# A bidirectional minGRU with a ternary feed-forward: order of the first loads, the place of one scale, the engine of small statistics, and the last steps

## The chip, the cores and the metric

The kernel runs on one core of one Trainium2 chip. The metric is the device time of one execution in microseconds (us); the figure shown is the median of several runs. Profiles come from one further, profiled execution.

## What is computed

The input x has shape (8, 512, 512): eight sequences b of 512 tokens with 512 features. The reference, cut to what matters:

```python
# _layernorm(v) has neither scale nor shift; all weights of the recurrence are ctx_1024[i], all biases cond_1024[i]
def mingru(x, W, b):                     # W, b serve for z and for h_tilde, in both directions
    z = sigmoid(x @ W.T + b);  h_tilde = tanh(x @ W.T + b)
    a = clip(1 - z, 1e-8, 1 - 1e-8)
    return linear_scan(a, z * h_tilde)   # h[s] = a[s] * h[s-1] + (z * h_tilde)[s]

def stack(x):                            # 4 layers
    h = x
    for i in range(4):
        h_new = mingru(h, ctx_1024[i], cond_1024[i])
        if i > 0: h_new = h_new + h
        h = layernorm(h_new) * gamma + beta
    return h

xn = _layernorm(x)
h = concat(stack(xn), flip(stack(flip(xn))))          # forward and backward in time
x = x + h @ fusion_W.T + fusion_b
y = _layernorm(x)
h = gelu(y @ absmean(W_fc).T)                         # 512 -> 2048, exact gelu
h = layernorm(h) * ln_w + ln_b                        # over the 2048
return x + h @ absmean(W_proj).T                      # 2048 -> 512
# absmean(W): sign(W) where |W| is over half the mean of |W|, 0 elsewhere
```

## The kernel before

**Layout.** P is 128. A sequence in the recurrence lies as features on partitions and its 512 tokens along the free dimension: four chunks of 128 features (NC_ = 4), each 128x512. Layer norms run over features, so a chunk group is turned by TensorE to four row tiles of 128 tokens (NT = 4), normalised, and turned back.

**One layer of one sequence and direction** (`layer`, L537). For each output chunk o: `gates` (L456) issues four matmuls into u (L461, 128x512, contracted over four input chunks); ScalarE makes a, t and z out of u (L478–L480); VectorE clips a (L484), multiplies z by t (L485) and scans (L489). For layers after the first the residual is added (L548 or L554). `norm` then queues two kinds of pieces: `turns`, four of them, each four transposes into a PSUM tile pt (L316, the pool of pt has two buffers), then `stats` and `normalise` (L168–L189) giving one token tile tok; and `backs`, four transposes of the four tok tiles into pf (L325), copied by ScalarE to h or x^T with gamma and beta (L331). After the last layer only the reciprocal deviation is taken (`norm_last`).

**Statistics of a row tile** (`stats`, `normalise`): bn_stats (L171) and bn_aggr (L173) on VectorE; ve = variance + eps (L177, VectorE); rs = ve to the power −0.5 (L178, GpSimd); nmu = −mean (L182, VectorE); nmr = nmu · rs (L188, ScalarE); tok = rs · src + nmr (L189, ScalarE). The same two functions serve for rows of x (rs alone), for the last layer (rs alone) and for rows of the feed-forward's input y.

**The first layer and x's own layer norm.** x is loaded twice: as rows (xn), for statistics, and transposed (x^T, `xT`), for the matmuls. The mean is taken out of the first weights instead of x: column means of the weights come from matmuls with ones into pm (L708), and four VectorE instructions subtract them from gw[0] (L711). The reciprocal deviations rx of a sequence are turned and spread by four transposes into pr (`scale_x`, L367) and copied by ScalarE to `scale` (L371). `first_layer` (L491) makes four chunks per sequence: four matmuls into u (L504); then, in a later stage, z = u · scale (L511), the factors, product, forward scan and backward scan. The statistics of a row can be made by ScalarE instead of VectorE (`second`, L375: two passes with accumulation, L380 and L382, one small operation between, and an end on VectorE and GpSimd, L385 and L386); `norm_x(b, at, scalar)` says for which rows.

**What sets the order.** The program order of each engine is written by hand (`manual_schedule`). `slot` (L439) is the unit: it issues the matmuls of one chunk, then the stages that are due ("factors", "late", "scans", "resid"), and between them shares of the queues `turns`, `backs`, `xturns` and `xbacks`; the ends of what they issued (normalise, copies to h) go last. A stage is put on the list with the slot number at which it is due (`now[0]` counts slots). [...]

**The start.** Twelve loads of 256 KB for sequence 0 go out from the queues of ScalarE and SyncE, first weights (`first_gw`), rows (`load_x`) and x^T (`first_xT`) mixed; then SyncE's queue issues the rest in turn. VectorE makes constants; two x rows' statistics are taken before the weights' fold (L711), the others after it. Chunk 0's matmuls are followed at once by pr (`with_scale`, L722).

**Feed-forward.** The weights have been made ternary during the recurrence. For each of 8 · 16 steps j, `fc(b, k)` makes 128 hidden features of one sequence (ph, gelu g, its square, high and low parts ghi and glo), sums g and its square for the layer norm, and two steps later `proj` adds them into four PSUM tiles po, one for each row tile. `token_stats(b)` turns the sums into rs and nmr per token (pow L882, nmrg L886). For the last sequence `center` (L896) adds the shift to the four rows before po is done, and `finish_last` (L915–L918) scales po, adds and stores one row tile; it is called after the last matmuls of each row tile. Near the end (L939) two steps issue `fc` twice, so that the last `proj` calls come row tile by row tile.

Of the kernel before, what the change touches and what calls it, by code (L numbers as in the profile page):

```python
# [24 lines left out]
def kernel(  # L25
# [68 lines left out]
    def load_x(use, b, t):  # L94
        xs[use, b, t] = xsp.tile([P, H], F32, tag="xs", name=f"x{use}_{b}_{t}")
        nc.sync.dma_start(out=xs[use, b, t], in_=x[b, ts(t, P), :])
# [10 lines left out]
    gb = const.tile([P, L, NC_], F32, name="gb")  # L107
    gam = const.tile([P, NC_], F32, name="gam")
    bet = const.tile([P, NC_], F32, name="bet")
    fb = const.tile([P, H], F32, name="fb")  # L110
    lnw = const.tile([P, NF], F32, name="lnw")
    lnb = const.tile([P, NF], F32, name="lnb")

# [2 lines left out]
    nc.vector.memset(warm, 0.0)  # L116
    ones = const.tile([P, P], F32, name="ones")
    nc.vector.memset(ones, 1.0)
    both = const.tile([P, NC_, 2, 64], F32, name="both")
    picks = []  # L120
    for i in range(2):
        s = const.tile([P, P], F32, name=f"fpick{i}")
        nc.vector.memset(s, 0.0)
        nc.vector.memset(s[64 * i : 64 * i + 1, :], 1.0 / H if i else 1.0)
        picks.append(s)
# [4 lines left out]
    def first_gw(q, c):  # L130
        q.dma_start(out=gw[0][:, c, :], in_=gru_wT[0][ts(c, P), :])

    def first_xT(q, c):
        q.dma_start(out=xT[0][:, c, :], in_=xt[0][ts(c, P), :])

    first_gw(nc.scalar, 0)
    load_x("n", 0, 0)
    first_gw(nc.scalar, 1)
    load_x("n", 0, 1)
    first_gw(nc.scalar, 2)  # L140
    first_gw(nc.sync, 3)
    first_xT(nc.scalar, 0)
    load_x("n", 0, 2)
    first_xT(nc.scalar, 1)
    load_x("n", 0, 3)
    for c in range(2, NC_):
        first_xT(nc.sync, c)
    nc.sync.dma_start(out=gb, in_=gru_b)
    for t in range(NT):
        load_x("n", 1, t)  # L150
# [17 lines left out]
    def stats(src, name, rs=None, shift=True):  # L168

        st = small.tile([P, 6], F32, tag="st", name=f"st_{name}")  # L170
        nc.vector.bn_stats(st, src)  # L171
        mv = small.tile([P, 2], F32, tag="mv", name=f"mv_{name}")
        nc.vector.bn_aggr(mv, st)  # L173
        if rs is None:
            rs = small.tile([P, 1], F32, tag="rs", name=f"rs_{name}")
        ve = small.tile([P, 1], F32, tag="ve", name=f"ve_{name}")
        nc.vector.tensor_scalar(ve, mv[:, 1:2], LN_EPS, None, ALU.add)  # L177
        nc.gpsimd.tensor_tensor(rs, ve, mhalf, ALU.pow)  # L178
        if not shift:
            return rs, None  # L180
        nmu = small.tile([P, 1], F32, tag="nmu", name=f"nmu_{name}")
        nc.vector.tensor_scalar(nmu, mv[:, 0:1], -1.0, None, ALU.mult)  # L182
        return rs, nmu

    def normalise(dst, src, rs_nmu, name):
        rs, nmu = rs_nmu
        nmr = small.tile([P, 1], F32, tag="nmr", name=f"nmr_{name}")
        nc.scalar.activation(nmr, nmu, AF.Copy, scale=rs)  # L188
        nc.scalar.activation(dst, src, AF.Identity, bias=nmr, scale=rs)  # L189

    def ternary(dst, w, hi_lo):
# [37 lines left out]
    with rec:  # L229
# [53 lines left out]
        def take(q):  # L283
            _, _, key, go = q.pop(0)
            left[key] -= 1
            return go()
# [104 lines left out]
        def norm_x(b, at, scalar=()):  # L391
            rx[b] = small.tile([P, NT], F32, tag="rsv", name=f"rx_{b}")
            for t in range(NT):
                queue(xturns, ("x", b), at + t, 0, second(b, t) if t in scalar else tokens(
                    lambda t=t: xs["n", b, t], None, rx[b][:, t : t + 1], f"x{b}_{t}"))
            queue(xbacks, ("x", b), at + NT + (2 if scalar else 1), 0, scale_x(b))
# [90 lines left out]
        def scan(dst, a, z, backward):  # L487
            d = slice(None, None, -1) if backward else slice(None)
            nc.vector.tensor_tensor_scan(dst[:, d], a[:, d], z[:, d], 0.0, ALU.mult, ALU.add)  # L489

        def first_layer(b, lag=0):  # L491


            zf, zb = [], []

            def chunk(o):
                def work():
                    while zlive[0] + 2 > ZT:
                        slot(None, 2)
                    zlive[0] += 2  # L500
                    name = f"{b}_0_{o}"
                    u = ps_u.tile([P, S], F32, tag="u", name=f"u_{name}")
                    for c in range(NC_):
                        nc.tensor.matmul(  # L504
                            u, lhsT=gw[0][:, c, ts(o, P)], rhs=xT[b][:, c, :],
                            start=(c == 0), stop=(c == NC_ - 1),
                        )

                    def scaled():
                        z = zp.tile([P, S], F32, tag="z", name=f"z_{name}")  # L510
                        nc.vector.tensor_tensor(z, u, scale[b], ALU.mult)  # L511
                        a, t = factors(z, z, 0, o, name)

                        def scans():
                            product(a, z, t)
                            f = zp.tile([P, S], F32, tag="z", name=f"zf_{name}")
                            scan(f, a, z, False)
                            zf.append(f)
                            if o == NC_ - 1:
                                state[b, 0] = xT.pop(b)  # L520
                                norm((b, 0), zf, f"{b}0_0", 2 if b == 1 else 1, 2 if b < 2 else 1)

                            def backward():
                                scan(z, a, z, True)
                                zb.append(z)
                                if o == NC_ - 1:
                                    norm((b, 1), zb, f"{b}1_0", 2 if b == 1 else 1, 2 if b < 2 else 1)
                            if b == 0:
                                stages.append((now[0] + 1, "resid", backward))
                            else:  # L530
                                backward()
                        stages.append((now[0] + 1, "scans", scans))
                    stages.append((now[0] + lag, "factors", scaled))
                return work
            return [chunk(o) for o in range(NC_)]

# [158 lines left out]
                load_x(use, b, t)  # L695


        norm_x(0, -2, (2,))
        norm_x(1, -2, (2, 3))
        for _ in range(2):  # L700
            take(xturns)

        idle = ps_t.tile([P, H], F32, tag="pt", name="idle")
        for _ in range(9):
# [5 lines left out]
            w = gw[0][:, c, :]  # L710
            nc.vector.scalar_tensor_tensor(w, pm0, -1.0 / H, w, ALU.mult, ALU.add)  # L711

        two = take(xturns)
        stages.clear()
        take(xturns)
        two()
        nc.vector.tensor_scalar(ngb, gb, -1.0, None, ALU.mult)
        take(xturns)
        f0, f1 = first_layer(0), first_layer(1, 2)
        first = f0[0]  # L720

        def with_scale():  # L722
            first()
            take(xbacks)()
        f0[0] = with_scale
        for i, work in enumerate(f0 + f1):
            slot(work, 4 if i == NC_ + 1 else 2, i > NC_ + 1)
        for i, v in enumerate((bet, gam)):
# [62 lines left out]


    gpool = ctx.enter_context(tc.tile_pool(name="g", bufs=3, reuse_waits="tile"))
    partp = ctx.enter_context(tc.tile_pool(name="parts", bufs=5, reuse_waits="tile"))
    accp = ctx.enter_context(tc.tile_pool(name="acc", bufs=1, reuse_waits="tile"))
    ps_x = ctx.enter_context(tc.tile_pool(name="ps_x", bufs=2, space=PSUM, reuse_waits="tile"))
    ps_o = ctx.enter_context(tc.tile_pool(name="ps_o", bufs=1, space=PSUM, reuse_waits="tile"))
# [116 lines left out]

    def finish_last(b, t):  # L915
        row = xs["y", b, t]
        nc.vector.scalar_tensor_tensor(row, po[b][t], stat[b][0][:, t : t + 1], row, ALU.mult, ALU.add)
        store(b, t)  # L918

    rests = []  # L920
    found, ytok = {}, {}
# [14 lines left out]
    for j in range(ends):  # L936
        b, k = divmod(j, NF)
        late = []
        for _ in range(2 if ends - 4 <= j < ends - 2 else 1):  # L939
            if todo:  # L940
                waiting.append((*todo[0], *fc(*todo[0])))
                todo.pop(0)
        if j == ends - 2:
            late.append(token_stats(b))
        if k == 0 and b > 0:
            late.append(token_stats(b - 1))
        if b == 0 and 5 <= k < 5 + NC_ + 3:
            row_piece(k - 5)
        if b + 1 < B and k >= NF - NC_:
            px = ps_x.tile([P, S], F32, tag="px", name=f"py_{b + 1}_{k}")  # L950
            late.append(y_chunk(b + 1, ytok[b + 1], k - (NF - NC_), px))
        if j >= LAG:
            done = waiting.pop(0)
            proj(*done)
        for f in late:
            f()
        if rests:
            rests.pop(0)()
        if j >= LAG and done[1] == NF - 1:
            finish(done[0])  # L960
        at = 12 if b == 0 else 8
        if at <= k < at + NT:
            xt = xs["y", b, k - at]
            nc.vector.tensor_tensor(xt, xt, rows[1], ALU.add)
        if b + 1 < B:
            if k == 2:
                load_y(b + 1)
            if k in (6, 7):
                y_stats(b + 1, (2 * k - 12, 2 * k - 11))
            if k in (8, 9):  # L970
                y_tokens(b + 1, (2 * k - 16, 2 * k - 15))
# [47 lines left out]
```

## Time and profile before

| what | value |
|---|---|
| median of 3 runs | 1719.33 us (1719.25 to 1719.43) |
| the profiled execution | 1719.44 us, its span 1717.4 us |
| instructions | 19766 |
| granted TensorE clock | 1.0 |
| pow of the statistics, L178 with tok following | 192 of them, median 655 ns, 548 to 1454 |
| nmr on ScalarE, L188 | 192, median 294 ns |
| tok on ScalarE, L189 | 192, median 777 ns |
| GpSimd's busy time | 214.5 us in 334 instructions |
| DMA | 91.75 MB, mean 53 GB/s |

The span is the time from the first to the last instruction that the profile shows; the time of an execution holds some 2 us more. Rows of the profile give line, engine, operation, out<-in by the program's names, shape, and how often; then busy time and the mean length of one. A timeline row gives start and length in us. A row of stretches gives the stretch, its length, and for PE, weight loads, VectorE, ScalarE and GpSimd the busy time and, in brackets, the number of instructions. A row of waits gives who waits for whom: us in total, times, longest.

### The profile page before, as it was taken

The numbers are of one execution on the slowest core, as the hardware profiler recorded it, in microseconds if no ns is written. First come the engines' busy times: TensorE is split into PE (matmuls) and PEld (weight loads), VectorE is DVE, ScalarE is ACT, GpSimd is POOL, SyncE is SP. The second block draws the span as 40 slices with busy tenths as digits, with TensorE's granted clock in tenths as the row PEclk, the third lists the DMA queues.
The fourth block names the chain that finished last, engine by engine and source line by source line (L and its number), as shares of the span: only waits on it lengthen the run. The fifth ranks groups of instructions, "written<-read, shape, count | busy, mean of one in ns | idle before, by whom it ended". The sixth has DMA issues, their size and how long they took to land.

```text
span 1717.4 us, 19766 instructions
## 1 busy us (share of the span) xinstructions
PE 1705.8 (99%) x6442; PEld 1042.8 (61%) x6442; DVE 1449.8 (84%) x2859; ACT 1072.3 (62%) x1851; POOL 214.5 (12%) x334
## 2 busy tenths in 40 slices
PE   9999999999999999999999999999999999999998
PEld 4455554555555455555545555554688888888887
DVE  7989989889998998999899899996568768768876
ACT  5898883468886246888624688861266566566654
POOL 2111111111111111111111111110000000000000
PEclk9999999999999999999999999999999999999999
DMA  7002221160000115000012200202201101100100
GB/s 270 19 25 81 99 86 43 56 202 1 1 13 19 56 59 199 1 1 19 13 55 68 105 15 35 74 1 98 74 1 49 50 1 50 50 19 32 50 19 31
DMA packets 46455, 91.75 MB, mean 53 GB/s; under 512 B 5264, under 2 KB 5264, under 8 KB 45328
## 3 DMA queue, kind: packets, MB, share of 16 engines
q1 hardware_dynamic: 45632, 89.18, 15.3%
q10 hardware_dynamic: 720, 1.31, 0.2%
q8 instruction: 51, 0.84, 0.2%
q14 instruction: 52, 0.43, 0.1%
HBM read 65.30 MB, written 25.17 MB: 53 GB/s over the span
## 4 chain that ended last, share of the span: by engine, by line
PE 85%; DVE 9%; issue 4%; ACT 1%; DMA 1%; POOL 0%; DVEq 0%; POOLq 0%; ACTq 0%; SPq 0%
PE u L461 33%; PE pu L582 12%; PE ph L836 12%; PE po L863 12%; PE pt L316 6%; PE u L504 5%; PE pf L325 4%; DVE z L489 2%; DVE st L171 1%; DVE z L485 1%; PE py L214 1%; DVE zf L489 1%; DVE z L548 1%; DVE a L484 1%; DMA xT<-in_xt_dram 0%
## 5 line engine op out<-in xcount | busy, mean ns | idle before, releaser
L461 PE MATMUL u<-h,gw 128*128 128x512 f32 x768 | 345.5, 592 | 0.0
L461 PE MATMUL u<-xT,gw 128*128 128x512 f32 x768 | 345.4, 593 | 0.0
L489 DVE TENSOR_TENSOR_SCAN z<-a,z 128x512 f32<-128x512 f32 x224 | 274.1, 1224 | 7.6
L840 ACT ACTIVATE g<-ph 128x512 f32<-128x512 f32 x128 | 76.4, 597 | 240.6 <-PE ph L836 240.6
L461 PEld LDWEIGHTS u<-h,gw 128*128 128x128 f32 x768 | 138.7, 190 | 139.2 <-issue 138.9
L461 PEld LDWEIGHTS u<-xT,gw 128*128 128x128 f32 x768 | 138.7, 190 | 139.2 <-issue 138.2
L478 ACT ACTIVATE a<-u,ngb 128x512 f32<-128x512 f32 x192 | 131.6, 685 | 142.2 <-PE u L461 141.6
L171 DVE BATCH_NORM_STATS2 st<-pt 128x6 f32<-128x512 f32 x256 | 177.1, 692 | 40.5 <-PE pt L316 40.1
L178 POOL TENSOR_TENSOR rs<-ve,mhalf 128x1 f32<-128x1 f32 x192 | 123.2, 642 | 702.8 <-DVE nmu L182 669.9
L863 PE MATMUL po<-pwq,ghi 128*128 128x512 f32 x512 | 203.5, 398 | 0.0
L836 PE MATMUL ph<-yhi,fcq 128*128 128x512 f32 x512 | 199.7, 390 | 0.0
L863 PE MATMUL po<-pwq,glo 128*128 128x512 f32 x512 | 199.6, 390 | 0.0
L836 PE MATMUL ph<-ylo,fcq 128*128 128x512 f32 x512 | 199.4, 389 | 0.0
L485 DVE TENSOR_TENSOR z<-z,t 128x512 f32<-128x512 f32 x224 | 153.4, 685 | 9.1 <-ACT z L480 9.1
L189 ACT ACTIVATE tok<-pt,nmr,rs 128x512 f32<-128x512 f32 x192 | 149.2, 777 | 6.4
L851 DVE TENSOR_TENSOR acc<-acc,g 128x512 f32<-128x512 f32 x112 | 77.3, 690 | 87.9 <-ACT g L840 87.0
L480 ACT ACTIVATE z<-u,gb 128x512 f32<-128x512 f32 x192 | 132.2, 689 | 0.0
L479 ACT ACTIVATE t<-u,gb 128x512 f32<-128x512 f32 x192 | 130.7, 681 | 0.0
L316 PEld LDWEIGHTS pt<-ident,z 128*128 128x128 f32 x640 | 78.6, 141 | 79.7 <-issue 47.7
L504 PE MATMUL u<-xT,gw 128*128 128x512 f32 x256 | 114.8, 593 | 0.8 <-DVE gw L711 0.8
L582 PE MATMUL pu<-fw,xT 128*128 128x512 f32 x256 | 115.2, 593 | 0.0
L582 PE MATMUL pu<-fw,h 128*128 128x512 f32 x256 | 115.1, 592 | 0.0
(147 smaller groups left out, 2558.5 us busy)
## 6 DMA issues: line engine op xcount, KB each, us to landing
xn<-in_x_dram SPq DMA_DIRECT2D x32, 256.0 KB, 4.4
xf<-in_x_dram SPq DMA_DIRECT2D x32, 256.0 KB, 5.5
x<-xf SPq DMA_DIRECT2D x32, 256.0 KB, 2.0
xy<-x SPq DMA_DIRECT2D x32, 256.0 KB, 4.4
out_dram<-xy SPq DMA_DIRECT2D x32, 256.0 KB, 2.0
xT<-in_xt_dram SPq DMA_DIRECT2D x7, 1024.0 KB, 7.5
fca<-in_fc_wT_dram SPq DMA_DIRECT2D x16, 256.0 KB, 3.0
pwa<-in_proj_wT_dram SPq DMA_DIRECT2D x16, 256.0 KB, 2.6
```

What stands on the lines that cost most here:

```text
L171: nc.vector.bn_stats(st, src)
L189: nc.scalar.activation(dst, src, AF.Identity, bias=nmr, scale=rs)
L316: nc.tensor.transpose(pt[:, ts(c, P)], zs[c][:, ts(t, P)], ident)
L461: nc.tensor.matmul(u, lhsT=gw[l][:, c, ts(o, P)], rhs=h[:, c, :], start=(c == 0), stop=(c == NC_ - 1),)
L478: nc.scalar.activation(a, u, AF.Sigmoid, bias=ngb[:, l, o : o + 1], scale=-1.0)
L480: nc.scalar.activation(z, u, AF.Sigmoid, bias=gb[:, l, o : o + 1])
L485: nc.vector.tensor_tensor(z, z, t, ALU.mult)
L489: nc.vector.tensor_tensor_scan(dst[:, d], a[:, d], z[:, d], 0.0, ALU.mult, ALU.add)
L504: nc.tensor.matmul(u, lhsT=gw[0][:, c, ts(o, P)], rhs=xT[b][:, c, :], start=(c == 0), stop=(c == NC_ - 1),)
L582: nc.tensor.matmul(pu, lhsT=hs[d][:, c, ts(t, P)], rhs=fw[:, d * NC_ + c, :], start=(c == 0), stop=(c == NC_ - 1),)
L836: nc.tensor.matmul(ph, lhsT=w, rhs=ys[b][c][i], start=(c == 0 and i == 0), stop=(c == NC_ - 1 and i == 1),)
L863: nc.tensor.matmul(po[b][t], lhsT=part[:, ts(t, P)], rhs=pwq[k // NP_][:, k % NP_, :], start=(k == 0 and i == 0), stop=(k == NF - 1 and i ...
```

## The change

There are five parts. The twelve first loads go out in another order: the four weight chunks first, then x^T and rows in pairs, in turn from ScalarE's and SyncE's queues. The statistics of x0's rows: rows 1 and 3 by ScalarE (before: row 2), rows 0 and 2 by VectorE, all issued after the weights' fold in program order; the scale's transposes and copy are issued within chunk 1, after its second matmul (`midway`), and chunk 0's factors one slot later (`wait`), so that its scans come in the same slot as they did. In `stats`, ve moves from VectorE to GpSimd, and nmu and nmr (VectorE and ScalarE) become one GpSimd instruction of two multiplications. In the tail, three steps instead of two issue `fc` twice, `token_stats` of the last sequence comes one step earlier, the "parts" pool has six buffers, and the last row tile is finished and stored in two halves, the second from ScalarE's queue. Three constants move to a pool that lives as long as the recurrence.

```diff
@@ -107,7 +107,7 @@
     gb = const.tile([P, L, NC_], F32, name="gb")
     gam = const.tile([P, NC_], F32, name="gam")
     bet = const.tile([P, NC_], F32, name="bet")
-    fb = const.tile([P, H], F32, name="fb")
+    fb = fusp.tile([P, H], F32, name="fb")
     lnw = const.tile([P, NF], F32, name="lnw")
     lnb = const.tile([P, NF], F32, name="lnb")
 
@@ -116,10 +116,10 @@
     nc.vector.memset(warm, 0.0)
     ones = const.tile([P, P], F32, name="ones")
     nc.vector.memset(ones, 1.0)
-    both = const.tile([P, NC_, 2, 64], F32, name="both")
+    both = fusp.tile([P, NC_, 2, 64], F32, name="both")
     picks = []
     for i in range(2):
-        s = const.tile([P, P], F32, name=f"fpick{i}")
+        s = fusp.tile([P, P], F32, name=f"fpick{i}")
         nc.vector.memset(s, 0.0)
         nc.vector.memset(s[64 * i : 64 * i + 1, :], 1.0 / H if i else 1.0)
         picks.append(s)
@@ -133,18 +133,14 @@
     def first_xT(q, c):
         q.dma_start(out=xT[0][:, c, :], in_=xt[0][ts(c, P), :])
 
-    first_gw(nc.scalar, 0)
-    load_x("n", 0, 0)
-    first_gw(nc.scalar, 1)
-    load_x("n", 0, 1)
-    first_gw(nc.scalar, 2)
-    first_gw(nc.sync, 3)
-    first_xT(nc.scalar, 0)
-    load_x("n", 0, 2)
-    first_xT(nc.scalar, 1)
-    load_x("n", 0, 3)
-    for c in range(2, NC_):
-        first_xT(nc.sync, c)
+    def first_rows(q, t):
+        xs["n", 0, t] = xsp.tile([P, H], F32, tag="xs", name=f"xn_0_{t}")
+        q.dma_start(out=xs["n", 0, t], in_=x[0, ts(t, P), :])
+
+    queues = (nc.scalar, nc.sync)
+    for load, at in ((first_gw, 0), (first_gw, 2), (first_xT, 0), (first_rows, 0), (first_xT, 2), (first_rows, 2)):
+        for i, q in enumerate(queues):
+            load(q, at + i)
     nc.sync.dma_start(out=gb, in_=gru_b)
     for t in range(NT):
         load_x("n", 1, t)
@@ -174,18 +170,16 @@
         if rs is None:
             rs = small.tile([P, 1], F32, tag="rs", name=f"rs_{name}")
         ve = small.tile([P, 1], F32, tag="ve", name=f"ve_{name}")
-        nc.vector.tensor_scalar(ve, mv[:, 1:2], LN_EPS, None, ALU.add)
+        nc.gpsimd.tensor_scalar(ve, mv[:, 1:2], LN_EPS, None, ALU.add)
         nc.gpsimd.tensor_tensor(rs, ve, mhalf, ALU.pow)
         if not shift:
             return rs, None
-        nmu = small.tile([P, 1], F32, tag="nmu", name=f"nmu_{name}")
-        nc.vector.tensor_scalar(nmu, mv[:, 0:1], -1.0, None, ALU.mult)
-        return rs, nmu
-
-    def normalise(dst, src, rs_nmu, name):
-        rs, nmu = rs_nmu
         nmr = small.tile([P, 1], F32, tag="nmr", name=f"nmr_{name}")
-        nc.scalar.activation(nmr, nmu, AF.Copy, scale=rs)
+        nc.gpsimd.tensor_scalar(nmr, mv[:, 0:1], rs, -1.0, ALU.mult, ALU.mult)
+        return rs, nmr
+
+    def normalise(dst, src, rs_nmr, name):
+        rs, nmr = rs_nmr
         nc.scalar.activation(dst, src, AF.Identity, bias=nmr, scale=rs)
 
     def ternary(dst, w, hi_lo):
@@ -488,6 +482,8 @@
             d = slice(None, None, -1) if backward else slice(None)
             nc.vector.tensor_tensor_scan(dst[:, d], a[:, d], z[:, d], 0.0, ALU.mult, ALU.add)
 
+        midway = {}
+
         def first_layer(b, lag=0):
 
 
@@ -505,6 +501,10 @@
                             u, lhsT=gw[0][:, c, ts(o, P)], rhs=xT[b][:, c, :],
                             start=(c == 0), stop=(c == NC_ - 1),
                         )
+                        if (b, o, c) in midway:
+                            midway.pop((b, o, c))()
+
+                    wait = 1 if (b, o) == (0, 0) else 0
 
                     def scaled():
                         z = zp.tile([P, S], F32, tag="z", name=f"z_{name}")
@@ -529,8 +529,8 @@
                                 stages.append((now[0] + 1, "resid", backward))
                             else:
                                 backward()
-                        stages.append((now[0] + 1, "scans", scans))
-                    stages.append((now[0] + lag, "factors", scaled))
+                        stages.append((now[0] + 1 - wait, "scans", scans))
+                    stages.append((now[0] + lag + wait, "factors", scaled))
                 return work
             return [chunk(o) for o in range(NC_)]
 
@@ -695,10 +695,8 @@
                 load_x(use, b, t)
 
 
-        norm_x(0, -2, (2,))
+        norm_x(0, -2, (1, 3))
         norm_x(1, -2, (2, 3))
-        for _ in range(2):
-            take(xturns)
 
         idle = ps_t.tile([P, H], F32, tag="pt", name="idle")
         for _ in range(9):
@@ -710,19 +708,14 @@
             w = gw[0][:, c, :]
             nc.vector.scalar_tensor_tensor(w, pm0, -1.0 / H, w, ALU.mult, ALU.add)
 
-        two = take(xturns)
+        for t in range(NT):
+            end = take(xturns)
+            if t % 2:
+                end()
         stages.clear()
-        take(xturns)
-        two()
         nc.vector.tensor_scalar(ngb, gb, -1.0, None, ALU.mult)
-        take(xturns)
+        midway[0, 1, 1] = lambda: take(xbacks)()
         f0, f1 = first_layer(0), first_layer(1, 2)
-        first = f0[0]
-
-        def with_scale():
-            first()
-            take(xbacks)()
-        f0[0] = with_scale
         for i, work in enumerate(f0 + f1):
             slot(work, 4 if i == NC_ + 1 else 2, i > NC_ + 1)
         for i, v in enumerate((bet, gam)):
@@ -791,7 +784,7 @@
 
 
     gpool = ctx.enter_context(tc.tile_pool(name="g", bufs=3, reuse_waits="tile"))
-    partp = ctx.enter_context(tc.tile_pool(name="parts", bufs=5, reuse_waits="tile"))
+    partp = ctx.enter_context(tc.tile_pool(name="parts", bufs=6, reuse_waits="tile"))
     accp = ctx.enter_context(tc.tile_pool(name="acc", bufs=1, reuse_waits="tile"))
     ps_x = ctx.enter_context(tc.tile_pool(name="ps_x", bufs=2, space=PSUM, reuse_waits="tile"))
     ps_o = ctx.enter_context(tc.tile_pool(name="ps_o", bufs=1, space=PSUM, reuse_waits="tile"))
@@ -914,8 +907,13 @@
 
     def finish_last(b, t):
         row = xs["y", b, t]
-        nc.vector.scalar_tensor_tensor(row, po[b][t], stat[b][0][:, t : t + 1], row, ALU.mult, ALU.add)
-        store(b, t)
+
+        for h in range(2 if t == NT - 1 else 1):
+            cols = slice(h * H // 2, (h + 1) * H // 2) if t == NT - 1 else slice(0, H)
+            nc.vector.scalar_tensor_tensor(
+                row[:, cols], po[b][t][:, cols], stat[b][0][:, t : t + 1], row[:, cols], ALU.mult, ALU.add
+            )
+            (nc.scalar if h else nc.sync).dma_start(out=out[b, ts(t, P), cols], in_=row[:, cols])
 
     rests = []
     found, ytok = {}, {}
@@ -936,11 +934,11 @@
     for j in range(ends):
         b, k = divmod(j, NF)
         late = []
-        for _ in range(2 if ends - 4 <= j < ends - 2 else 1):
+        for _ in range(2 if ends - 6 <= j < ends - 3 else 1):
             if todo:
                 waiting.append((*todo[0], *fc(*todo[0])))
                 todo.pop(0)
-        if j == ends - 2:
+        if j == ends - 3:
             late.append(token_stats(b))
         if k == 0 and b > 0:
             late.append(token_stats(b - 1))
```

## The prediction

> **What bounds the kernel now.** I read the shares of busy time first, then the chain that ended last, then PE's waits, then stretches.
>
> ```profile
> PE 1705.8 (99%) x6442; PEld 1042.8 (61%) x6442; DVE 1449.8 (84%) x2859; ACT 1072.3 (62%) x1851; POOL 214.5 (12%) x334
> ...
> PE 85%; DVE 9%; issue 4%; ACT 1%; DMA 1%; POOL 0%; DVEq 0%; POOLq 0%; ACTq 0%; SPq 0%
> ```
>
> TensorE works for 1705.8 of 1717.4 us, and none of its work is changed. So the change can win only what PE loses, and can lose whatever makes PE wait. The stretches show where it loses (us, then busy time of each engine):
>
> ```profile
> 0.00:18.00 18.00, 15.89 (x46) 8.96 (x47) 9.07 (x29) 5.37 (x11) 3.98 (x12) 1.00 0.93 317
> 18.00:45.00 27.00, 25.35 (x86) 12.74 (x84) 24.59 (x50) 18.75 (x36) 5.52 (x9) 1.00 0.60 218
> 45.00:90.00 45.00, 42.94 (x157) 22.55 (x157) 42.87 (x87) 37.98 (x69) 5.30 (x9) 1.00 0.06 18
> ...
> 390.00:530.00 140.00, 140.00 (x517) 75.83 (x517) 128.08 (x264) 113.75 (x194) 23.00 (x36) 1.00 0.03 10
> ...
> 1700.00:1718.00 18.00, 13.00 (x61) 10.26 (x59) 11.45 (x22) 3.63 (x6) 1.01 (x1) 0.96 0.16 60
> ```
>
> From 18 to 90 us PE loses 1.65 + 2.06 = 3.7 us, and DVE is at 91% and 95%: that stretch is DVE's. From 390 to 530 PE loses nothing. The last 18 us lose 5.0. PE's own waits:
>
> ```profile
> PE pt L316 <- ACT tok L189: 2.5, 7, 0.6
> PE pt L316 <- DVE z L489: 1.3, 1, 1.3
> ...
> PE u L504 <- DVE gw L711: 0.8, 1, 0.8
> ...
> PE pf L325 <- ACT tok L189: 0.4, 1, 0.4
> ```
>
> The commonest is for tok, the end of the statistics chain that the change rebuilds. Its steps in a slot of the steady part (start, duration):
>
> ```profile
> 436.44 0.18 DVE L173 BATCH_NORM_AGGREGATE mv<-st 128x2 f32<-128x6 f32 x1
> 436.73 0.15 DVE L177 TENSOR_SCALAR ve<-mv 128x1 f32<-128x1 f32 x1
> 436.80 0.14 DVE L182 TENSOR_SCALAR nmu<-mv 128x1 f32<-128x1 f32 x1
> 436.86 0.42 DVE L484 TENSOR_SCALAR a<-a 128x512 f32<-128x512 f32 x1
> 437.19 0.68 DVE L485 TENSOR_TENSOR z<-z,t 128x512 f32<-128x512 f32 x1
> 437.91 1.23 DVE L489 TENSOR_TENSOR_SCAN z<-a,z 128x512 f32<-128x512 f32 x1
> ```
>
> On POOL the pow runs 437.03–437.68, then on ACT nmr 437.71–438.00 and tok 438.04–438.82. A slot of PE (16 matmuls and eight transposes) is 4.31 us; ACT idles 0.76 of it.
>
> [...] L178's pow takes 0.548 us alone or beside the bn_stats, 0.656 when L484 runs, 0.967 when it starts under L485, and 1.454 under the scan L489. In each blocked case it ends 0.41 after the DVE instruction does; DVE is not stretched (L485 0.684 against 0.687). [...] the trace has none on POOL; its neighbours are a 128x1 memset, 0.10, and the pow, 0.55. [...] the second pm matmul took 0.873, later ones 0.429.
>
> **The change part by part.** Sum against the profiled execution, 1719.44 (span 1717.4 and 2.0 around it), 0.11 above the median of 1719.33.
>
> *Loads.* g0–g3 land at 4.91, 6.18, 7.84 and 7.15 before; landings come about 0.6 apart whatever the queue, so as the first four they come by some 6.6. The pm matmuls then go at PE's pace: PE's 0.22 wait goes and u0 starts about 10.2 instead of 10.65: −0.5 (bounds 0 and −0.8[...]). x's rows land up to 2 us later; their statistics have until 15 us. SP's later loads (gb, xn1, x^T of 1) keep their bytes ahead, so do not move.
>
> *The scale inside chunk u1.* x's transposes leave the gap before u1; the two extra ACT statistics (x0's row 1 and row 3) end near 15.7, so pr waits about 0.3, and chunk 0's factors come a slot later. ACT's statistics of x1's rows 2 and 3 (L380–L382, 1.7 to 2 us a row) slide behind the factors of chunks 2 and 3: x1's row 3 ends near 30 instead of 26.7, x1's scale at about 31.5 instead of 29.2. What is queued behind it on DVE and PE are chunks of x1, whose products feed the DVE-bound stretch. Against that DVE is spared ve and nmu: mv to next st is 0.43, of which about 0.21 goes, for 28 statistics up to 90 us, 5.9 in all. The burst of four statistics at 35–41 us goes through POOL with three operations each. I take the first 90 us at +2 after the start, bounds −3.7 (all that PE loses there) and +6 (2.3 of scale, and 3.7 if the burst also grows).
>
> *Statistics.* Per token statistic POOL gets ve and nmr (192 + 64 + 32 + 29 pows become two or three operations), DVE loses 0.14 and 0.15, ACT 0.29. ACT and DVE are not the bound after 90 us, so their gain is nothing there; latency is. Before, from mv's end: ve+pow+nmr = 436.62 to 438.00, 1.38. After, for a POOL tensor_scalar I take 0.34 (bounds 0.10, the memset, and 0.55, the pow), with 0.15 for the handover from DVE and from step to step: 0.15+0.34+0.15+0.55+0.15+0.34 = 1.68, so tok is 0.3 to 0.4 later when nothing blocks. In the slot above it does block: L484 starts earlier and holds ve until about 437.1, L485 then holds the pow to 437.87+0.41 = 438.28, the scan L489 holds nmr to 439.13+0.2, and tok ends 440.17: D = 1.35 later. Then ACT is half a microsecond late, L485 too, and the pow of the next slot gets in ahead of it. I take D = 0.85, the middle of 0.35 and 1.35.
>
> What is late next: PE's transposes of tok into h or x^T (L325). The slack from tok's end to the transpose that needs it, for the last tok of each group: about 1.32 in some 25 groups (no loss), and 0.73, 0.51, 0.53, 0.05, 1.15, 0.05 from 115 to 230 us, 0.89 three times (405.7, 703.9, 1002.1), 0.72, 0.05, 0.05, 0.24 later. At D = 0.85 the shortfalls are 0.12+0.34+0.32+0.80+0.80+0.13+1.60+0.61 = +4.7; at 0.35 they are 1.3, at 1.35 they are 10.8 and 0.03 for each of the 25, 11.6.
>
> Where two tokens fall into one slot, the second is later still: 0.8 with nothing blocked, 1.5 with product and scan behind it; I take 1.15. There the pt tiles (two buffers) wait for tok's reading: slack 0.05 at 332.9 and at 374.7, and again near 631, 673, 929 and 971. 1.1 at each of the six, +6.6 (bounds 0, if DVE's earlier start takes it up, and 6 × 1.45 = 8.7). From 100 to 128 us one such pair has slack 0.25: +0.9 (0 to 2).
>
> *FFN statistics* (32 y rows) have microseconds to spare: 0, hidden by the fc matmuls; uncovered it would be D a row. *Pools* fb, both and fpick, and a sixth "parts" buffer: 0.
>
> *Tail.* DVE runs L896 and L917 to 1714.29 behind the pow that ended at 1708.68; PE ends about 1713.0. With token_stats a step earlier L896 is done before PE ends, and the last row's finish in halves, the second stored from ACT's queue, saves about half of 0.68 and 0.3 of DVE's lateness: −0.7 (0 to −1.5). The extra fc costs nothing, being the same matmuls; uncovered, one GELU group behind it would be 0.6.
>
> Sum: −0.5 + 2 + 0.9 + 4.7 + 6.6 − 0.7 = +13.0, so 1732.4, and 1732.3 by the median. With the first 90 us at nothing, D at 0.35 and the pairs at 0.75 it is −0.5 + 0 + 0.4 + 1.3 + 4.5 − 1.0 = +4.7, 1724; with all bad ends 0 + 6 + 2 + 11.6 + 8.7 = +28.3, 1747.7. All good ends, −4.7, are the ground of rival C.
>
> **Rivals.** B: GpSimd's small operations are near 0.1, the chain fits its slack, and only start and tail remain, −1.2: 1718.2. For it: 0.10 for the memset, 1.32 of slack in most groups. Against it: the pow's 0.55 on the same 128x1[...]. C, the other side: DVE's relief in 18–90 us decides. DVE is spared up to 5.9 us where it is the bound and PE loses 3.7; with start and tail 1719.4 − 0.5 − 3.7 − 0.7 = 1714.5. It decides from the point where the chain grows by less per statistic than the 0.21 that DVE is spared there, since then the pt waits ("ACT tok L189: 2.5, 7") shrink rather than grow. For it: 95% of DVE at 45–90. Against it: x1's scale comes later and the burst is serial on POOL. D: every chain is blocked and ACT's 0.76 is used up, leaving 1.35 − 0.76 = 0.59 in half of the 128 steady statistics: 38 us, 1757. Against it: a late ACT makes L485 late and lets the pow in.
>
> **How the numbers follow.** Forecast A 0.50, B 0.20, C 0.23, D 0.07. About 0.2%, 3.4 us, is what a measurement of this kernel can tell from no change: 1715.9 to 1722.8. C is faster, B within, A and D slower: 0.23, 0.20, 0.57. The range from 1713 to 1748 takes in A, B and C with its better ends (1714.5, less 0.3 at the start and 0.8 in the tail), and leaves out D and about 0.1 in all at the ends. A's own range is 1724 to 1748.
>
> **What would show it.** On POOL: tensor_scalar of 0.2 to 0.5 us, pows of 0.97 and 1.45 more often than before, nmr ending with the scan. Waits "PE pf L325 <- ACT tok" of 0.8 near 192, 227, 526 and 824, and "PE pt" of about 1 near 333 and 375. PE busy 42.9 or less in 45–90 for A, 44 or more for C. ACT's tok should then wait for POOL's nmr, and its a (L478) for u less than 141.6 us. I am wrong if the tensor_scalar takes 0.1, if the pow gets in ahead of L485 in most slots, or if PE's gaps after 90 us don't grow.

## The result, and the profile after

The changed kernel takes 1740.2 us (median of 4 runs, 1740.1 to 1741.13) against 1719.37 before: a ratio of 1.0122, interval 1.0105 to 1.014. It is slower by 20.8 us where 13.0 were forecast; the time lies in the range of forecast A (1724 to 1748). The profiled execution took 1740.26 us, its span is 1738.5 us, at a granted clock of 0.998.

The page's first lines and its chain:

```profile
PE 1709.4 (98%) x6442; PEld 1044.1 (60%) x6442; DVE 1394.3 (80%) x2318; ACT 1011.7 (58%) x1632; POOL 476.7 (27%) x874
...
PE 59%; issue 21%; POOL 14%; DVE 4%; ACT 2%; POOLq 0%; DVEq 0%
```

VectorE lost 56 us of work, ScalarE 61, and GpSimd gained 262, in a good part of which it stood blocked (below). POOL had 0% of the chain that ended last and has 14% now, though it is only 27% busy. ("issue" is time for which the profile shows no wait.) PE's waits:

```profile
PE pt L310 <- ACT tok L183: 12.4, 14, 2.0
PE pf L319 <- ACT tok L183: 7.8, 8, 2.3
PE pr L361 <- POOL rx L380: 2.4, 1, 2.4
```

The waits for tok were 2.5 and 0.4; they are 20.2 now. The 17.3 us more are most of the loss of 20.8. tok itself waits for nmr, in ScalarE's waits:

```profile
ACT tok L183 <- POOL nmr L178: 200.8, 176, 7.6
```

and GpSimd's instructions of the chain take these times (rows of groups: count, then busy us and mean ns):

```profile
L174 POOL TENSOR_TENSOR rs<-ve,mhalf 128x1 f32<-128x1 f32 x192 | 148.6, 774 | 16.0
L178 POOL TENSOR_SCALAR nmr<-mv,rs 128x1 f32<-128x1 f32 x192 | 106.1, 553 | 19.9
L173 POOL TENSOR_SCALAR ve<-mv 128x1 f32<-128x1 f32 x256 | 78.5, 307 | 732.8 <-DVE mv L169 710.4 <-ACT z L474 17.6 <-ACT t L473 2.6
```

Unblocked, nmr takes 0.27 us and ve 0.22, so half of nmr's 0.553 is waiting. The stretches, beside those of before:

```profile
18.00:45.00 27.00, 22.98 (x78) 11.75 (x77) 22.26 (x38) 16.52 (x31) 9.81 (x22) 0.96 0.58 211
45.00:90.00 45.00, 42.19 (x140) 21.69 (x139) 39.16 (x62) 33.02 (x56) 11.29 (x22) 0.95 0.06 18
...
390.00:530.00 140.00, 140.00 (x519) 76.03 (x518) 121.23 (x198) 105.25 (x163) 59.28 (x100) 1.00 0.04 14
```

In 45–90 VectorE is freed (87% busy instead of 95%), and PE is busy less than before, not more. The column before the DMA share is PE's granted clock: 0.96 and 0.95, where it was 1.00. From 390 to 530 PE still loses nothing: the longer chain fits there.

Where each microsecond is lost can be read by laying the same PE instruction of both traces side by side; the difference of its start grows in steps:

| PE instruction (time before) | late by, us | step |
|---|---|---|
| chunk u1, first matmul (14.86) | −1.67 | start: −1.0 at u0, and pr no longer ahead of u1 |
| pr of x1 (28.9) | +1.30 | +2.97: x1's scale |
| pt after the first pairs (87.2) | +6.05 | +4.75: tok, and a granted clock of 0.5 |
| pt (101.1) | +7.47 | +1.42 |
| pf (120.0, 137.6, 192.8) | +11.87 | +1.36, +1.42, +1.61 |
| pr (227.8) | +11.28 | −0.59 |
| pt of the second pair of sequences (374.7) | +13.83 | +2.55 |
| the third pair (672.9) and the fourth (971.1) | +16.50, +19.22 | +2.67, +2.72 |
| pf (1125.7) | +21.72 | +2.50 |
| the end of the span | +21.1 | −0.6: tail |

One of the three alike steps, at the second pair (timeline, start and length):

```profile
383.78 0.18 DVE L169 BATCH_NORM_AGGREGATE mv<-st 128x2 f32<-128x6 f32 x1
383.88 0.39 DVE L478 TENSOR_SCALAR a<-a 128x512 f32<-128x512 f32 x1
384.19 0.68 DVE L479 TENSOR_TENSOR z<-z,t 128x512 f32<-128x512 f32 x1
384.42 0.59 POOL L178 TENSOR_SCALAR nmr<-mv,rs 128x1 f32<-128x1 f32 x1
384.91 1.22 DVE L483 TENSOR_TENSOR_SCAN z<-a,z 128x512 f32<-128x512 f32 x1
...
385.09 1.06 POOL L173 TENSOR_SCALAR ve<-mv 128x1 f32<-128x1 f32 x1
...
386.17 0.69 DVE L548 TENSOR_TENSOR z<-z,xT 128x512 f32<-128x512 f32 x1
386.24 1.05 POOL L174 TENSOR_TENSOR rs<-ve,mhalf 128x1 f32<-128x1 f32 x1
...
387.39 0.27 POOL L178 TENSOR_SCALAR nmr<-mv,rs 128x1 f32<-128x1 f32 x1
...
388.52 0.66 PE L310 MATMUL pt<-ident,z 128*128 128x128 f32 x4 [1.99 <-ACT tok L183]
```

Two statistics fall into one slot. The first one's nmr gets in as the product ends. The second one's ve (0.22 when free) stands under the scan for 1.06, its pow under the residual add for 1.05, and PE waits 2 us for the pt tile that this tok has yet to read. From mv's end (383.96) to nmr's end it is 3.70 us.

### The profile page after: what moved, and what is told of

It reads as the page before. It is cut to its first block, busy times and chain, and to the rows that moved or that the text cites. A ratio compares the mean times of both kernels' runs of the same rounds, so it can differ in the third digit from the quotient of the medians.

```text
span 1738.5 us, 19489 instructions
## 1 busy us (share of the span) xinstructions
PE 1709.4 (98%) x6442; PEld 1044.1 (60%) x6442; DVE 1394.3 (80%) x2318; ACT 1011.7 (58%) x1632; POOL 476.7 (27%) x874
## 4 chain that ended last, share of the span: by engine, by line
PE 59%; issue 21%; POOL 14%; DVE 4%; ACT 2%; POOLq 0%; DVEq 0%
PE u L455 18%; PE po L856 13%; PE ph L829 13%; POOL rs L174 6%; PE pu L582 5%; POOL nmr L178 4%; PE pt L310 3%; PE u L500 3%; POOL ve L173 3%; PE pf L319 2%; PE py L208 1%; ACT tok L183 1%; DVE zf L483 1%; DVE z L483 1%; POOL ve_x L173 0%
## 5 line engine op out<-in xcount | busy, mean ns | idle before, releaser
L173 POOL TENSOR_SCALAR ve<-mv 128x1 f32<-128x1 f32 x256 | 78.5, 307 | 732.8 <-DVE mv L169 710.4
L472 ACT ACTIVATE a<-u,ngb 128x512 f32<-128x512 f32 x192 | 131.3, 684 | 96.4 <-PE u L455 95.8
L174 POOL TENSOR_TENSOR rs<-ve,mhalf 128x1 f32<-128x1 f32 x192 | 148.6, 774 | 16.0
L844 DVE TENSOR_TENSOR acc<-acc,g 128x512 f32<-128x512 f32 x112 | 77.5, 692 | 91.6 <-ACT g L833 90.7
L319 PE MATMUL pf<-ident,tok 128*128 128x128 f32 x768 | 113.4, 273 | 8.1 <-ACT tok L183 7.8
```

What stands on the lines that cost most here:

```text
L319: nc.tensor.transpose(pf[:, ts(t, P)], toks[t][:, ts(c, P)], ident)
L472: nc.scalar.activation(a, u, AF.Sigmoid, bias=ngb[:, l, o : o + 1], scale=-1.0)
```

## The experiments

All chain lengths below are measured in the same way: from the end of mv to the end of its tok, over the 192 token statistics. Before: mean 2.28 us, 5 over 3 us, 2 over 3.5 us. After: 2.95, 89 and 25.

**Which part.** First the statistics alone, then all but the statistics.

```diff
 before.py, with stats and normalise of after.py
-        nc.vector.tensor_scalar(ve, mv[:, 1:2], LN_EPS, None, ALU.add)
+        nc.gpsimd.tensor_scalar(ve, mv[:, 1:2], LN_EPS, None, ALU.add)
...
-        nc.vector.tensor_scalar(nmu, mv[:, 0:1], -1.0, None, ALU.mult)
-        nc.scalar.activation(nmr, nmu, AF.Copy, scale=rs)
+        nc.gpsimd.tensor_scalar(nmr, mv[:, 0:1], rs, -1.0, ALU.mult, ALU.mult)
```

> The kernel before with only the statistics moved to GpSimd (ve, and one nmr there for nmu and ScalarE's nmr); loads, scale and tail as before. Theory (the longer chain on GpSimd[...] makes PE wait for tok): nearly the whole loss, about 1739 us, with waits of PE for tok of some 20 us as in the changed kernel. Rival (the new head, with the scale inside chunk 1 and x1's scale late, is what costs): about 1722 us.

1738.77 us, ratio 1.0113 (1.0098 to 1.0129). As the theory had it, and its waits of PE are those of the changed kernel:

```profile
PE pt L314 <- ACT tok L187: 12.4, 15, 2.0
PE pf L323 <- ACT tok L187: 8.1, 8, 2.6
```

```diff
 after.py, with stats and normalise of before.py (the edit above, the other way)
```

> The changed kernel with the statistics of before (ve and nmu on VectorE, nmr on ScalarE). Theory: head -1.7 (PE's second chunk in the changed trace starts that much earlier), +2.5 for PE's wait for x1's scale, tail -0.6: about 1719.6 us. Rival (the head costs): 1735 us or more.

1721.33 us, ratio 1.0012 (1.0005 to 1.0019). Close to the theory, 1.7 us above it, and far from the rival's 1735. The wait for x1's scale is there (2.6 us), and the start's gain does not pay for it. Statistics +19.3 and the rest +1.8 add up to 21.1, near the whole 20.8.

**Which of the two moves.**

```diff
 before.py, e3
-        nc.vector.tensor_scalar(ve, mv[:, 1:2], LN_EPS, None, ALU.add)
+        nc.gpsimd.tensor_scalar(ve, mv[:, 1:2], LN_EPS, None, ALU.add)
 before.py, e4
-        nc.vector.tensor_scalar(nmu, mv[:, 0:1], -1.0, None, ALU.mult)
-        nc.scalar.activation(nmr, nmu, AF.Copy, scale=rs)
+        nc.gpsimd.tensor_scalar(nmr, mv[:, 0:1], rs, -1.0, ALU.mult, ALU.mult)
```

> The kernel before with ve alone on GpSimd, nmu on VectorE and nmr on ScalarE as before. VectorE's next instruction (L484) starts earlier and the pow falls under the product or the scan. Theory [...]: half or more of the loss, about 1728 us, with pows of 0.97 to 1.45 us more often. Rival (only the number of GpSimd instructions in the chain counts, about 0.3 us each): the same as moving nmr alone, within 2 us of the next kernel.

> The kernel before with ve on VectorE as before, and nmr as one GpSimd instruction for nmu and ScalarE's nmr. Theory [...]: the pow keeps its place ahead of the product, nmr falls into the gap between product and scan in most slots, so a small loss, about 1722 us. Rival (only the number of GpSimd instructions counts): within 2 us of the kernel with ve alone on GpSimd.

ve alone: 1722.0, ratio 1.0014 (1.0008 to 1.0021). nmr alone: 1717.94, ratio 0.9992 (0.9984 to 1.0001), 1.5 us under before, at the edge of what can be told. I had both too high. The rival, that only the number of GpSimd instructions counts, fails: each kernel has one more, and they lie 4.1 us apart, not within 2. The surprise is the sum: +2.5 and −1.5 apart, +19.3 together. Chains over 3 us: 10 and 8 apart, 89 together; with nmr alone the mean chain is even shorter than before, 2.20 us. A steady slot of the kernel with nmr alone shows why:

```profile
436.00 0.42 DVE L482 TENSOR_SCALAR a<-a 128x512 f32<-128x512 f32 x1
...
436.24 0.59 POOL L178 TENSOR_TENSOR rs<-ve,mhalf 128x1 f32<-128x1 f32 x1 [3.36 <-DVE ve L177]
436.35 0.69 DVE L483 TENSOR_TENSOR z<-z,t 128x512 f32<-128x512 f32 x1
436.92 0.27 POOL L182 TENSOR_SCALAR nmr<-mv,rs 128x1 f32<-128x1 f32 x1
437.08 1.23 DVE L487 TENSOR_TENSOR_SCAN z<-a,z 128x512 f32<-128x512 f32 x1
```

And one of the kernel with ve alone:

```profile
433.42 0.51 POOL L177 TENSOR_SCALAR ve<-mv 128x1 f32<-128x1 f32 x1 [2.82 <-DVE mv L173]
433.44 0.42 DVE L484 TENSOR_SCALAR a<-a 128x512 f32<-128x512 f32 x1
...
433.79 0.69 DVE L485 TENSOR_TENSOR z<-z,t 128x512 f32<-128x512 f32 x1
434.02 0.89 POOL L178 TENSOR_TENSOR rs<-ve,mhalf 128x1 f32<-128x1 f32 x1
434.52 1.22 DVE L489 TENSOR_TENSOR_SCAN z<-a,z 128x512 f32<-128x512 f32 x1
```

Between mv and the scan VectorE changes instruction twice, after the clip and after the product, and in these two slots a GpSimd instruction gets in at each change: with nmr alone the pow ends 0.41 us after the clip and nmr 0.15 after the product, with ve alone ve ends 0.07 after the clip and the pow 0.43 after the product. Two GpSimd instructions find two openings. A third one stands under the scan of 1.22 us, as here in the changed kernel:

```profile
446.67 0.69 DVE L479 TENSOR_TENSOR z<-z,t 128x512 f32<-128x512 f32 x1
446.70 1.09 POOL L174 TENSOR_TENSOR rs<-ve,mhalf 128x1 f32<-128x1 f32 x1
447.40 1.22 DVE L483 TENSOR_TENSOR_SCAN z<-a,z 128x512 f32<-128x512 f32 x1
447.89 0.80 POOL L178 TENSOR_SCALAR nmr<-mv,rs 128x1 f32<-128x1 f32 x1
```

Of its 192 nmr 63 start in this way under a scan; they take 0.797 us in the mean, and each ends 0.07 us after the scan.

**Length without GpSimd.** Two idle copies on ScalarE lengthen every chain by about as much as the mean grew, with no further GpSimd instruction.

```diff
 before.py, normalise
         nc.scalar.activation(nmr, nmu, AF.Copy, scale=rs)
+        for _ in range(2):
+            more = small.tile([P, 1], F32, tag="nmr", name=f"more_{name}")
+            nc.scalar.activation(more, nmr, AF.Copy)
+            nmr = more
```

> The kernel before with two more 128x1 copies on ScalarE between nmr and tok: every chain gets some 0.66 us longer, about the mean lengthening in the changed kernel (2.28 to 2.95 us from the end of mv to the end of tok), but evenly[...]. The copies do no other work. Theory (the chains that the scan blocks on GpSimd, over 3 us long, do the harm, the even part mostly fits the slack of 1.3 us): about 1727 us, less than half of the loss. Rival (the mean length of the chain sets the loss): about 1739 us.

1738.18 us, ratio 1.0108 (1.0093 to 1.0124): the rival's number, and my expectation failed. The mean chain is 2.91 us. The waits say how:

```profile
PE pt L320 <- ACT tok L193: 12.6, 21, 0.8
PE pf L329 <- ACT tok L193: 6.3, 8, 2.7
```

The total is that of the changed kernel, in more and shorter pieces (21 of at most 0.8 instead of 14 of at most 2.0). Where two statistics share a slot ScalarE runs both chains in turn (from 381.2 to 384.3 us nmr, two copies and tok of one, then of the other), so the second is late twice over. It isn't ScalarE's work as such: from 390 to 530 us PE loses nothing in this kernel either. So GpSimd isn't needed for a loss of this size: a chain that is 0.63 us longer in the mean costs nearly as much when ScalarE makes it long. What the waiting on GpSimd does is to make the chain that long (2.95 us in the mean for 2.28). The mean alone is no law: ve alone has a mean of 2.61, half of the way, and costs 2.5 us, not 9. Nor are the chains over 3 us, of which this kernel has 43 against 89. Those over 3.5 us go with the loss best: 24 here, 25 and 26 in the two kernels with both moves, which all lose 18.7 to 20.8 us; 3 and 2 with one move alone, 2 before. That is a reading of six kernels, all with two pt tiles, and no test.

**The factor a in PSUM.** The clip and the scan then have an operand there, and the scan reads one input from SBUF where it read two.

```diff
-        ps_u = rec.enter_context(tc.tile_pool(name="ps_u", bufs=4, space=PSUM))
+        ps_u = rec.enter_context(tc.tile_pool(name="ps_u", bufs=3, space=PSUM))
+        ps_a = rec.enter_context(tc.tile_pool(name="ps_a", bufs=1, space=PSUM))
...
-                a, t = factors(u, z, l, o, name)
+                a, t = factors(u, z, l, o, name, ps_a)      # in gates alone
```

> Control: the kernel before with the factor a of layers 2 to 4 in PSUM (one bank; u has three banks instead of four), so that there the scan, and the clip ahead of it, have a PSUM operand, and the scan only one SBUF input. Chunks of the first layer keep a in SBUF. No theory of the statistics expects more here than what one bank less of u costs: 1719 to 1724 us.

> The same with the statistics on GpSimd (ve and nmr), loads and tail as before. Theory [...]: ve and nmr of 1.06 to 1.18 us are gone in layers 2 to 4, and of the 19 us that the same edit costs with a in SBUF less than 8 are left over the control. Rival (the bare length of three GpSimd instructions in a row): 15 us or more over the control.

The control took 1750.63 (ratio 1.0181, 1.0166 to 1.0196), far over the 1719 to 1724 that I gave it: the clip in PSUM takes 0.652 us in the mean instead of 0.417, a has one tile where it had three in SBUF, and ScalarE's a now waits for the scan (161.9 us) where it waited for u (141.6). My expectation left both out. With the statistics on GpSimd it took 1728.96 (ratio 1.0057, 1.004 to 1.0073): the same edit that costs 19.3 us with a in SBUF gains 21.7 here. As a difference of times the pair is no clean test, since the control is bound elsewhere. The durations say more:

```profile
L178 POOL TENSOR_TENSOR rs<-ve,mhalf 128x1 f32<-128x1 f32 x192 | 111.0, 578 | 16.2 <-POOL ve L177 0.2
L177 POOL TENSOR_SCALAR ve<-mv 128x1 f32<-128x1 f32 x256 | 67.1, 262 | 840.5 <-DVE mv L173 816.0 <-ACT z L479 6.9 <-PE pr L366 6.1
L182 POOL TENSOR_SCALAR nmr<-mv,rs 128x1 f32<-128x1 f32 x192 | 57.3, 298 | 19.8
```

The same three instructions with a in SBUF (the first experiment):

```profile
L178 POOL TENSOR_TENSOR rs<-ve,mhalf 128x1 f32<-128x1 f32 x192 | 149.2, 777 | 16.1 <-POOL ve L177 0.2
L182 POOL TENSOR_SCALAR nmr<-mv,rs 128x1 f32<-128x1 f32 x192 | 105.9, 552 | 19.9
L177 POOL TENSOR_SCALAR ve<-mv 128x1 f32<-128x1 f32 x256 | 78.3, 306 | 733.4 <-DVE mv L173 714.8 <-ACT z L478 13.8 <-ACT t L477 2.6
```

nmr falls from 0.552 to 0.298, the pow from 0.777 to 0.578, close to their free lengths. In 14 of the statistics pow and nmr both lie wholly under one scan:

```profile
376.06 1.22 DVE L488 TENSOR_TENSOR_SCAN z<-a,z 128x512 f32<-128x512 f32 x1
376.19 0.57 POOL L178 TENSOR_TENSOR rs<-ve,mhalf 128x1 f32<-128x1 f32 x1
376.86 0.26 POOL L182 TENSOR_SCALAR nmr<-mv,rs 128x1 f32<-128x1 f32 x1
```

With a in SBUF no nmr of the changed kernel that starts under a scan ends before it. The mean chain is 2.39 instead of 2.96 and 23 are over 3 us instead of 89. Shown by this is that beside a scan and a clip with an operand in PSUM GpSimd's instructions are no longer held (nmr 0.26 us under that scan, 0.80 under the scan of the changed kernel); how much time that is worth on its own is not, and why the edit gains as much as 21.7 us over this control was not taken apart.

**The waits at pt.** A third pt tile, for one u less:

```diff
-        ps_u = rec.enter_context(tc.tile_pool(name="ps_u", bufs=4, space=PSUM))
-        ps_t = rec.enter_context(tc.tile_pool(name="ps_t", bufs=2, space=PSUM))
+        ps_u = rec.enter_context(tc.tile_pool(name="ps_u", bufs=3, space=PSUM))
+        ps_t = rec.enter_context(tc.tile_pool(name="ps_t", bufs=3, space=PSUM))
```

> The changed kernel with three pt tiles instead of two, and three u instead of four. Theory (12.4 of the 20 us are PE's transposes waiting for a pt tile that tok has yet to read): those waits fall to 3 us or less and the time to about 1731 us, if one u less costs nothing. Rival (the chain's delay is throughput of GpSimd and ScalarE, and a buffer only moves the wait to the transposes back): 1738 us or more.

1728.91 us (ratio to before 1.0055, 1.004 to 1.007), 11.3 us under the changed kernel, though its chains are no shorter (mean 2.99):

```profile
PE pf L319 <- ACT tok L183: 7.1, 8, 2.3
PE pu L582 <- DVE xf L592: 3.0, 2, 1.5
...
PE pt L310 <- ACT tok L183: 0.2, 1, 0.2
```

The pt waits fall from 12.4 to 0.2; those of pf, which need the values of tok, stay at 7.1; one u less brings 3.0 for pu, which shares u's tiles. So the rival (a lack of throughput, 1738 us or more) fails: at pt the delay is latency, which a third tile takes up.

**Head and tail.** The tail alone:

```diff
 before.py
-        for _ in range(2 if ends - 4 <= j < ends - 2 else 1):
+        for _ in range(2 if ends - 6 <= j < ends - 3 else 1):
...
-        if j == ends - 2:
+        if j == ends - 3:
 and finish_last, the parts pool and the three constants as in after.py
```

> The kernel before with the tail of the changed one alone (three doubled fc, token_stats a step earlier, last row tile in halves, six parts buffers, the pools). Theory: -0.6 us, 1718.8. Rival (the store that ends the execution is what counts and halves don't shorten it): no change, 1719.4.

1719.13 us, ratio 0.9998 (0.9989 to 1.0007): −0.3, which can't be told from nothing. The step of −0.6 in the table is that of one trace. Then the head, with one line more:

```diff
 after.py with stats of before.py, and
+        take(xturns)
         midway[0, 1, 1] = lambda: take(xbacks)()
```

> The changed kernel with the statistics of before, and one more share of x1's statistics (its row 0) issued ahead of the first chunk, as the kernel before had it, so that ScalarE's two rows of x1 come one slot earlier. Theory (the head loses by PE's wait of 2.6 us for x1's scale alone): the wait goes, and 1717.5 to 1718.5 us. Rival (the wait only moves to x1's chunks or to the first pt): 1720 or more.

1719.79 us, ratio 1.0002 (0.9994 to 1.0011). PE's wait for x1's scale goes and the time falls by 1.5 us from 1721.33, but not to the theory's 1717.5 to 1718.5. The rival has it: PE's pt waits for scans grow instead (1.8 and 0.6 where before there was 1.3). At its second chunk PE is 2.1 us ahead of the kernel before; at the pt of 39.4 us 0.3 are left.

**The best found.** The mended head, the tail, and nmr alone on GpSimd (the edits of b0 above, with stats as in the kernel with nmr alone):

> The same head and tail, with nmr alone on GpSimd and ve on VectorE. Theory (the gains add: -1.5 for nmr, about -1.5 for head and tail): 1716 to 1717 us, under both kernels. Rival (nmr's gain comes from the relief of the first 90 us and is the same gain as the head's): 1718 us.

1716.84 us, ratio 0.9985 (0.9978 to 0.9992): 2.6 us under before, the only version that is clearly faster than both kernels. The number is the theory's, its sum is not: head and tail gave +0.35 by themselves and not the −1.5 that it took, so −1.2 with nmr's −1.5. Where the rest comes from is open, and it is near what can be told.

And the same with the third pt tile:

> The kernel with nmr alone on GpSimd and the mended head and tail, with three pt and three u. It has 1.8 us of waits of pt for tok left. Theory: 1715 to 1716 us. Rival (u needs its fourth tile): 1718 us or more.

1719.19 us, ratio 0.9999 (0.9991 to 1.0008): the rival's number. With short chains a third pt has little to give (its waits for tok fall from 1.8 to 0.4), and with three u tiles PE waits 3.6 us for pu.

## Why the prediction was right, and where its terms were off

**The case.** Forecast A happened: the chain on GpSimd is late, and PE waits. Most signs named for it are there: ve of 0.22 to 0.3 us, pows and nmrs that end with a product or scan, PE at 42.19 (under 42.9) in 45–90, ScalarE's a waiting for u 95.8 us instead of 141.6. Of the 192 pows 63 start under a product and 59 while VectorE stands idle, so the pow does get in early in many slots, and the middle that I took for D fits. Of the six places named, 375 (1.8 us) and 192 (1.6) show near twice the forecast; 333 gives 0.4, 526 and 824 give 0.2, 227 nothing. That 20.8 us still lie in the range owes much to its width: the upper end took in 28.3. B fails by the first experiment. C fails too: VectorE did get its relief (busy 39.2 us of 45), but the chain grew by 0.67 us in the mean, more than the 0.21 spared, the point below which C would have decided. D was refuted by 390–530, where PE loses nothing.

**Start, −0.5: measured −1.7 at the second chunk.** u0 came 1.0 us earlier, not 0.5, and pr no longer stood in front of u1, for which I had put down nothing.

**First 90 us, +2: measured +7.7 from that start,** over my upper bound of 6. This is the term that was mis-sized most. x1's pr was 1.3 us late where I had 2.3 for the scale, which from the earlier start is the step of 2.97; the burst and the first pairs cost the rest, and about 3 us of it, by my estimate from the matmuls' starts below, is a thing that the forecast didn't have: a granted clock of 0.5. The trace shows it for 3.4 us from 43.0 us and again from 80.6 us, and the records of u lie up to 0.86 us apart instead of 0.43, four from 43.1 and three from 81.6 us. A row of six u instructions over 4.40 us:

```profile
42.46 0.85 PE L319 MATMUL pf<-ident,tok 128*128 128x128 f32 x5 [0.78 <-ACT tok L183]
43.10 4.40 PE L500 MATMUL u<-xT,gw 128*128 128x512 f32 x6
```

What brings it is not shown. Both stretches follow waits for tok (1.7 us in three pieces from 39.6 us, 2.5 in two from 77.5), but with single waits of 1.99 us up to 388.5 and of 2.34 up to 1147.4 the trace has no such stretch. No run here took the waits away and left the rest. Nor is this clock what makes the loss: the kernel with two copies more on ScalarE lost 18.7 us with a granted clock of 1.00 throughout from 0 to 530 us, and a mean of 0.999 over its whole span.

**100 to 128 us, +0.9: measured +1.42.** Right in kind.

**Tight groups, +4.7: measured +3.8 up to 228 us, some 0.4 at 526 and 824, and +2.5 at 1125.7, 6.7 in all.** D in the mean was 0.67, under my 0.85, but the groups with shortfalls were others: 0.05 of slack at 227.7 cost nothing, as the chain was short there, and the last one cost 2.5 for my 0.61; y's statistics (norm_y) stand just ahead of it on GpSimd and ScalarE, but no run took them apart. So it is in part luck that the sums are as near as 4.7 and 6.7. Slacks of one trace say where a delay can hurt, not which chain will be the long one.

**Pairs, +6.6: measured +7.9 in the three turns,** less some 0.4 that belongs to the groups: 7.5. The places, 333 and 375 us and their repeats, were right; the split was not (0.42 at the first, about 2.1 at the second).

**Tail, −0.7: measured −0.6 in the trace, −0.3 by itself.** (The 5.0 us that the forecast has PE lose in the last 18 hold 0.6 us past the end of the span at 1717.4.) FFN statistics and pools cost nothing, as said.

The sum was 13.0, measured 21.1 in the span; of the 8 missing, 4.5 are start and first 90 us taken together, and 2 the group at 1125.7.

**GpSimd beside VectorE.** That ve and nmr would be held as the pow was in the trace of before was my estimate, and the traces bear it out: nmr takes 0.27 us free, 0.80 when it starts under a scan with both inputs in SBUF, 0.26 under one with a in PSUM. VectorE was not stretched (product 0.689 against 0.685, scan 1.224 both). One reading was off: under the scan the one pow of before ended 0.34 us after it, not 0.41.

## What to carry to other kernels

Count the openings before moving small instructions to GpSimd. Here, in slots with clip, product, scan and residual add one behind the other, all in SBUF, they got in where VectorE changed from one to the next (each of the 63 nmr of 0.27 us that took 0.80 ended 0.07 us after the scan under which it started), so two moves together cost what neither did alone (−1.5 and +2.5 apart, +19.3 together). Relief for an engine that is 84% busy was worth nothing where PE waits for a latency chain with a two-tile buffer behind it (in 45–90 VectorE went from 95% to 87%, and PE from 42.94 to 42.19 us); look at the places where two chains share a slot, for there the second was the late one (PE waited 1.99 us for it). And read the granted clock after such waits: here it was 0.5 for 3.4 us twice, and u's matmuls started up to 0.86 us apart instead of 0.43.

## What the runs showed of the hardware that was not expected

- A GpSimd tensor_scalar on 128x1 takes 0.22 us with a constant (ve) and 0.27 with a scale from a tile (nmr): at most half of the pow's 0.55 to 0.57, and in the lower half of my range of 0.10 to 0.55.
- That the scan holds a GpSimd instruction as a product does was forecast: a 0.22 us ve took 1.06 under it. That it does not with a in PSUM (nmr 0.26 under it), and that its own time stays 1.22, was not.
- The clip a<-a has one tensor input and holds a GpSimd instruction too while it lies in SBUF (136 ve that start under it end 0.08 us after it); in PSUM it does not (129 of the 132 that start under it alone end within it, at 0.22 us).
- The clip a<-a costs 0.65 us in PSUM instead of 0.42 in SBUF.
